# The head of a conditioned residual kernel in another order: sums over x ahead of the condition copies, x weight's sums early

## The chip, the cores and the metric

The kernel runs on one core of a Trainium2 chip. The metric is the device time of one execution in microseconds (us); before the change three runs gave 977.57, 976.78 and 973.87, median 976.78. A core has five engines that run their own instruction lists in order and wait for each other by semaphores: PE (TensorE, matrix products), DVE (VectorE), ACT (ScalarE), POOL (GpSimd) and SP (SyncE, which here only starts transfers). POOL starts the indexed transfers (gathers of rows and the scatter of the output), SP the others.

## The reference, cut to what matters

```python
h = _ln(x, pw_g[pathway_ids], pw_b[pathway_ids])
h = _ln(h, cp_g[compartment_ids], cp_b[compartment_ids])
t = _ln(x, tm_g[time_steps], tm_b[time_steps])
m = x + _mlp_ln(memory_state, ...)[:, None, :]
n = x + _mlp_ln(noise_state, ...)[:, None, :]
r = x + _mlp_ln(resource_state, ...)[:, None, :]
s = _ln(x, ms_g[scale_type], ms_b[scale_type])
w = jax.nn.softmax(aw)
cat = jnp.concatenate([w[0]*h, w[1]*t, w[2]*m, w[3]*n, w[4]*r, w[5]*s], axis=-1)
return x + _mlp_ln(cat, int_W1, int_b1, int_W2, int_b2, int_g, int_be)
```

x has 16 x 512 tokens of 512 values, all in float32. `_mlp_ln` is silu(s W1 + b1) W2 + b2 with a layer norm behind it; for m, n and r its input has one row for each of the 16 batches ("conditions").

## The kernel before

**What it makes of the reference.** The product with `int_W1` is split by the six blocks of `cat`. The x in m, n and r goes through one weight, wx_ = w2 W1[2] + w3 W1[3] + w4 W1[4]; t and s are the same normalized x with different row tables, so they go through one weight that depends on a token's group (time step and scale type: 15 groups). For that the kernel sorts all tokens by group, and takes them in 16 tiles of 512 tokens, each of four rows g of 128. What a token adds by its group and batch is a row of a small table, gathered and added. Rows of 128 tokens in which two groups meet are put right by "extra" tiles e0 and e1, whose products change those table rows.

**Stages.** First come loads, index arithmetic and a sort's loop of one-hot products (L815 to L819), up to about 33 us of the trace. Behind that loop everything is done in *pieces*, short closures with names, and three strings say in which order they are issued: `ORDER` for the head (conditions, tables, extra tiles, all of tile 0 and the most of tiles 1 and 2), `WINDOW` once for each tile, and `LAST`. The order in a string is the order of the instructions on every engine, since the schedule is by hand (`tc.manual_schedule()`, L501). `run` (L1212) takes the names one after the other:

```python
for name in names.split():
    ...
    if name not in done:
        done.add(name)
        piece(name)
```

A name is `kind.tile.index`; `e0` and `e1` stand for the extra tiles. The kinds that the text uses, with their lines and engines:

- `gx` (L200, POOL) gathers 128 rows of x into `xbs`; tile 0's four gathers come ahead of `ORDER` (L845). `gh` (L205, POOL) gathers a row of `pw` and one of `cp`.
- `xs` (L233, ACT) two passes over 128 rows of x for mean and variance, `xe` (L242, DVE), `xp` (L246, POOL) the power of -0.5 into `rsx`, `xm` (L254, DVE) `nmx`. `xn`, `nv` (L278, L272, ACT) the normalized x.
- `f1`, `fp`, `f2`, `fn`, `th` (L281 to L305) the second layer norm for h on DVE, POOL, DVE, ACT, and its transpose into `rH`; `tv`, `tx` the transposes into `rV`, `rX` (all DVE, L182). `sV.w.g`, `sH`, `sX`, `sZ`, `sE` (L187, SP): four transfers that spread row g of a transposed tile into `cV`, `cH`, `cX`, `cZ`, `cEe`. The transposed tile of e0 shares its room with `rX`.
- `xt`, `xv` (L951, L957): for tile 0, x is transposed on PE and copied by DVE.
- `sp` (L213, ACT) and `bd` (L222, DVE): the weight `vs` of row g, each four instructions; there are two such buffers.
- `lX`, `lV`, `lH` (L315, PE, products at L320): layer 1 of row g, one group of products for each block; `ga`, `ha`, `hs`, `tz` gather what is added, add, silu, transpose; `l2` (L336, PE) layer 2.
- `h2.s` (L964, PE) the second products of condition s, `he.s` (L969, ACT) their copies, `eh.s` (L978, PE) sums of quarters, `cv` (L1017, PE) the condition vectors `pv`; then `cs` (L1022, DVE), `cp` (L1029, POOL, `rsc`), `cn` (L1037, DVE), `ct` (L1040, PE), `ca` (L1045, DVE).
- `wk.s.c` (L947, DVE) adds block c of the x weight's part s into `wx_`. `lh` (L880, SP) loads `wh_`, `wh` (L995, ACT) scales it; `lw` (L1161, SP) loads `w2`; `lt` (L876, SP) three small tables.
- `tb`, `cm` (L1008, L1050, PE): products into `pb`, the table of additions; `cr` (L1057, ACT) copies it, `rp`, `rc`, `ro` pick and store its rows. `dp`, `dc`, `do` make the difference rows that `gr` gathers for the extra tiles; `mt`, `tr` (DVE) multiply and transpose them.
- `sz`, `scl` (L983, L1003): scales of the tiles on PE and ACT. `ax`, `ac`, `pwi`, `bx`, `by`, `kd`, `px`, `tk`: indices.
- `ex.k` (L1107, PE, `pe`) an extra product, `ea.k` (L1113, POOL, `adde`) the rows to be changed, `ee.k` (L1117, DVE) their sum, `eo.k` (L1120, SP) its storing. `xa` (L1070, DVE) and `ar` (L1128, DVE, 16 small instructions) make indices for `ea` and `ga`.

**What holds an instruction back.** Its operands, a free buffer (four PSUM slots for most of the head's small products, three for `pw` and for `cp`), and whatever stands ahead of it in its engine's list. A gather on POOL that waits for a buffer stops the powers behind it as well.

Of the kernel before, what the change touches and what calls it, by code (L numbers as in the profile page):

```python
# [17 lines left out]


ORDER = """  # L20
    sz scl bx lt ax wk.1.3 h2.1 ac sp.0.0 h2.2 lh he.2 cv h2.0 he.0 wk.1.1 pk se eh.2 eh.0 lw by pwi kd px dk he.1
    eh.1 wk.1.0 gh.0.2 xs.0.1 xs.0.0 dp wk.1.2 tk xt.0.2 xt.0.3 cg gh.0.0 gh.0.1 xs.0.3 xt.0.1 cs wk.2.2 xv.0.2
    xt.0.0 cp gx.e1.3 gx.e0.1 tt wk.2.0 cn xs.0.2 xv.0.3 xe.0 xv.0.1 dc wh gx.e1.2 xp.0 xv.0.0 ct xm.0 xn.0.2
    gx.e0.0 ca f1.0.2 nv.0.1 xn.0.1 wk.2.1 tb fp.0.2 cm do xn.0.0 wk.2.3 lX.0.1 gx.e0.2 f2.0.2 f1.0.0 fp.0.0 nv.0.2
    fn.0.2 xs.e0.1 xn.0.3 lo lX.0.3 tv.0.2 nv.0.0 nv.0.3 th.0.2 gh.0.3 lX.0.0 tv.0.1 cr rp.1 f2.0.0 fn.0.0 f1.0.1
    tv.0.0 tv.0.3 xs.e0.0 fp.0.1 f2.0.1 th.0.0 xs.e0.2 sp.0.1 gx.e0.3 xs.e0.3 gr.e0.2 sV.0.2 f1.0.3 gx.e1.0 fp.0.3
    lX.0.2 bd.0.1 f2.0.3 gx.e1.1 sV.0.1 fn.0.1 rp.0 xe.e0 th.0.1 fn.0.3 xp.e0 xs.e1.3 gr.e0.3 th.0.3 xs.e1.0 xm.e0
    nv.e0.3 sV.0.0 bd.0.0 gr.e0.0 sV.0.3 mt.e0.3 tr.e0.3 xa sH.0.1 nv.e0.2 mt.e0.2 rc.1 xs.e1.2 lV.0.1 xs.e1.1 xe.e1
    lV.0.0 tr.e0.2 gr.e0.1 gx.1.2 nv.e0.0 mt.e0.0 lH.0.1 nv.e0.1 rc.0 sp.0.3 sH.0.0 xp.e1 gr.e1.0 sH.0.3 xm.e1
# [22 lines left out]
    lV.c.1 sZ.p.3 q7.p.0.1 f1.c.2 f2.c.2 lX.c.3 xs.n.0 gx.n.2 f2.c.3 gx.n.3 fp.c.3 sp.c.2 fn.c.3 bd.c.2 fp.c.2  # L52
    fn.c.2 q7.p.0.2 sZ.p.2 po.o.2 sZ.p.1 sh.c.1 tx.n.1 ga.c.2 th.c.2 zs.p.4 xs.n.2 lV.c.2 xs.n.3 xe.n th.c.3 zs.p.5
    q7.p.1.5 sp.c.3 bd.c.3 tx.n.2 sH.c.1 q7.p.1.1 lV.c.3 lH.c.1 xp.n xm.n xn.n.0 nv.n.0 po.o.3 tx.n.0 kf.p.0 sp.n.0
    kf.p.2 zs.p.6 kf.p.3 zs.p.0 sH.c.0 zs.p.1 nv.n.3 ga.c.1 q7.p.1.7 sH.c.3 zs.p.7 sp.n.1 q7.p.1.3 sH.c.2 zs.p.2
    tx.n.3 nv.n.1 ga.c.0 q7.p.1.6 ku.p.1 tv.n.0 f1.n.0 ha.c.1 q7.p.0.5 sX.n.2 q7.p.1.2 q7.p.0.6 tv.n.3 sf.p.3 tv.n.1
    bd.n.0 zs.p.3 sf.p.2 gh.n.1 ga.c.3 sX.n.3 kf.p.1 fp.n.0 sf.p.0 q7.p.1.4 nv.n.2 xn.n.1 q7.p.0.7 sl.p.2 tv.n.2
    lH.c.0 sl.p.3 lq.p.2 sf.p.1 hs.c.1 ku.p.0 q7.p.0.4 gh.n.2 lq.p.3 f1.n.1 f2.n.0 sh.c.2 ha.c.0 q7.p.0.3 fn.n.0
    hs.c.0 sX.n.0 sX.n.1 sl.p.0 sh.c.0 sl.p.1 lq.p.0 sV.n.1 fp.n.1 th.n.0 f2.n.1 tz.c.0 lq.p.1 sh.c.3 lv.p lH.c.2
    ha.c.2 fn.n.1 lH.c.3 lp.p th.n.1 tz.c.1 lb.p.0 hs.c.2 sV.n.0 gh.n.3 sV.n.2 po.p.0 lb.p.2 lb.p.1 gx.m.0 gx.m.1  # L60
    po.p.1 sV.n.3
# [12 lines left out]
"""


# [1210 lines left out]
```

## Time and profile before

| what | before |
|---|---|
| runs | 973.87, 976.78, 977.57 us |
| span of the profiled execution | 973.856 us (the page shows no time beside the span) |
| granted TensorE clock, mean | 0.990 |
| PE busy | 946.2 us, 97% |
| DVE / POOL / ACT busy | 861.0 / 658.9 / 569.6 us |
| HBM read / written | 102.31 / 19.94 MB |

Times in the views are microseconds from the span's start. A row of the timeline reads: start, time, engine, line, operation, written tile <- read tiles, shapes, number of instructions, and in brackets the idle time of the engine just before and what ended it. Where several semaphores were waited for, the one that came last in the profile is named. A row of the windows reads: stretch, length, busy time and (instructions) of PE, PEld (weight loads), DVE, ACT, POOL, the granted clock as a share of full speed, the busy share of the DMA engines, GB/s. The chain of waits follows the work that ended last back in time; a row of it reads start, time, what.

### The profile page before, as it was taken

How to read it: one execution, taken by the hardware profiler on the slowest of the kernel's cores; microseconds unless marked ns; L12 is line 12 of the kernel's file. 1: busy time of each engine (PE TensorE's matmuls, PEld its weight loads, DVE VectorE, ACT ScalarE, POOL GpSimd, SP SyncE). 2: the span in 40 equal slices, each digit the busy share in tenths (PEclk: the TensorE clock that was granted, in tenths of full speed). 3: DMA queues.
4: the chain of work that ended last, by engine and by line, in shares of the span. 5: the costliest groups of instructions: out<-in, count | busy, mean ns of one | idle time of the engine just before them, and what ended most of it. 6: DMA issues, size and time to landing. Idle time of an engine off the chain costs nothing.

```text
span 973.9 us, 11591 instructions
## 1 busy us (share of the span) xinstructions
PE 946.2 (97%) x2901; PEld 497.9 (51%) x2901; DVE 861.0 (88%) x1412; ACT 569.6 (58%) x1190; POOL 658.9 (68%) x697
## 2 busy tenths in 40 slices
...
GB/s 278 207 255 218 283 244 244 135 223 206 203 203 180 196 173 193 195 202 197 207 200 188 196 173 193 205 197 184 205 204 208 202 180 179 199 194 166 148 85 97
DMA packets 91885, 190.95 MB, mean 196 GB/s; under 512 B 25364, under 2 KB 25364, under 8 KB 91820
## 3 DMA queue, kind: packets, MB, share of 16 engines
...
q14 instruction: 41, 0.34, 0.1%
...
HBM read 102.31 MB, written 19.94 MB: 126 GB/s over the span
## 4 chain that ended last, share of the span: by engine, by line
PE 79%; DVE 11%; DMA 4%; ACT 3%; SPq 2%; issue 2%; POOLq 0%; ACTq 0%; DVEq 0%
PE p L320 57%; PE p L339 4%; PE pq_1b L406 4%; DVE vs L226 4%; PE pq_0b L406 4%; PE pq_0a L406 3%; PE pq_1a L406 3%; SPq L192 2%; PE pe L1110 1%; DMA cX<-rX 1%; DVE yb L433 1%; DVE vs L724 1%; ACT junk L238 1%; DMA cZ<-rZ 1%; DMA cH<-rH 1%
## 5 line engine op out<-in xcount | busy, mean ns | idle before, releaser
L320 PE MATMUL p<-wh__83,cH 128*128 128x512 f32 x512 | 227.3, 592 | 1.0 <-DMA cH<-rH 1.0
L320 PE MATMUL p<-wx__82,cX 128*128 128x512 f32 x512 | 224.9, 592 | 0.0
L320 PE MATMUL p<-vs,cV 128*128 128x512 f32 x504 | 223.7, 592 | 0.8 <-DVE rH L184 0.8
L226 DVE SCALAR_TENSOR_TENSOR vs<-wt,sct,vs 128x512 f32<-128x512 f32 x252 | 214.5, 912 | 0.0
L220 ACT ACTIVATE vs<-ws,scs 128x512 f32<-128x512 f32 x252 | 161.3, 710 | 3.4 <-PE p L320 2.4
L320 PEld LDWEIGHTS p<-wx__82,cX 128*128 128x128 f32 x512 | 97.2, 190 | 117.3 <-issue 111.3
L320 PEld LDWEIGHTS p<-wh__83,cH 128*128 128x128 f32 x512 | 97.2, 190 | 112.7 <-issue 107.8
L320 PEld LDWEIGHTS p<-vs,cV 128*128 128x128 f32 x504 | 95.7, 190 | 110.5 <-issue 87.1
L497 POOL DMA_INDIRECT out<-yb,tok x64 | 71.0, 1110 | 59.9 <-DVE yb L462 20.7
L292 POOL TENSOR_TENSOR rsh<-veh,mhalf 128x1 f32<-128x1 f32 x64 | 51.0, 798 | 75.9 <-DVE veh L288 75.1
L471 ACT ACTIVATE junk<-yb 128x512 f32<-128x512 f32 x64 | 40.4, 631 | 96.9 <-DVE yb L435 78.4
L158 POOL DMA_INDIRECT cp<-cp_rows,i_cp x64 | 68.7, 1073 | 27.4 <-issue 18.0
L327 ACT ACTIVATE add<-add 128x512 f32<-128x512 f32 x64 | 39.8, 622 | 80.5 <-DVE add L324 80.4
L158 POOL DMA_INDIRECT xbs<-in_x,tok x64 | 66.9, 1046 | 24.5 <-issue 15.7
L158 POOL DMA_INDIRECT add<-rows,i_add x64 | 70.3, 1098 | 17.3 <-issue 10.8
L309 POOL TENSOR_TENSOR xbs<-xbs,rows 128x512 f32<-128x512 f32 x64 | 80.7, 1272 | 0.7
L158 POOL DMA_INDIRECT pw<-in_pw,i_pw x64 | 66.3, 1035 | 18.0 <-issue 11.0
L238 ACT ACTIVATE junk<-xbs 128x512 f32<-128x512 f32 x72 | 45.2, 628 | 56.4 <-DMA xbs<-in_x,tok 54.9
L296 ACT ACTIVATE pw<-pw,rsh 128x512 f32<-128x512 f32 x64 | 44.5, 715 | 55.1 <-POOL rsh L292 26.9
L260 ACT ACTIVATE xn<-xbs,nmx,rsx 128x512 f32<-128x512 f32 x64 | 50.2, 804 | 45.3 <-DVE nmx L256 44.8
L324 DVE TENSOR_TENSOR add<-p,add 128x512 f32<-128x512 f32 x64 | 43.7, 685 | 29.5 <-PE p L320 25.1
L260 ACT ACTIVATE xm<-xbs,nmx,rsx 128x512 f32<-128x512 f32 x64 | 51.9, 810 | 13.9 <-DVE rV L184 11.8
...
## 6 DMA issues: line engine op xcount, KB each, us to landing
cV<-rV SPq DMA_DIRECT2D x256, 64.0 KB
cH<-rH SPq DMA_DIRECT2D x256, 64.0 KB
cZ<-rZ SPq DMA_DIRECT2D x256, 64.0 KB
...
```

Source lines behind the costliest of these rows:

```text
L158: nc.gpsimd.indirect_dma_start(dst, None, table, bass.IndirectOffsetOnAxis(ap=idx, axis=0), **kw)
L220: nc.scalar.activation(v[:, c], ws[:, c], AF.Identity, scale=scs[:, c, g, w : w + 1])
L226: nc.vector.scalar_tensor_tensor(v[:, c], wt[:, c], sct[:, c, g, w : w + 1], v[:, c], ALU.mult, ALU.add)
L238: nc.scalar.activation(junk, x, AF.Identity, accum_out=sums[:, 0, j : j + 1])
L260: nc.scalar.activation(t, st["xb"][:, j, :], AF.Identity, bias=st["nm"][:, j : j + 1], scale=st["rs"][:, j : j + 1])
L292: nc.gpsimd.tensor_tensor(rs, st.pop(("ve", j)), mhalf[:, :1], ALU.pow)
L296: nc.scalar.mul(pw[:, :D], pw[:, :D], st.pop(("rs", j)))
L309: nc.gpsimd.tensor_add(st["xb"][:, j, :], st["xb"][:, j, :], rows[:, 2, :])
L320: nc.tensor.matmul(st["p1", g], st["c" + blk][:, g, c, :], m[:, c, :], start=(blk == "X" and c == 0), stop=(blk == "H" and c == NC - 1))
L324: nc.vector.tensor_add(st["add", g], st["p1", g], st["add", g])
L406: nc.tensor.matmul(home, st["zp", p][k][:, c], at_["half"][k][:, c], start=False, stop=(c == 1), skip_group_check=True)
L497: nc.gpsimd.indirect_dma_start(out_rows, bass.IndirectOffsetOnAxis(ap=tok[:, j, w : w + 1], axis=0), yb[:, j, :], None)
```

## The change

`ORDER` gets another order of the same 427 names: none is added or taken away. `WINDOW` and `LAST` hold the same names in the same order as before and are only broken into lines elsewhere, which moves the line numbers behind them by one. Both orders in full:

```diff
-    sz scl bx lt ax wk.1.3 h2.1 ac sp.0.0 h2.2 lh he.2 cv h2.0 he.0 wk.1.1 pk se eh.2 eh.0 lw by pwi kd px dk he.1
-    eh.1 wk.1.0 gh.0.2 xs.0.1 xs.0.0 dp wk.1.2 tk xt.0.2 xt.0.3 cg gh.0.0 gh.0.1 xs.0.3 xt.0.1 cs wk.2.2 xv.0.2
-    xt.0.0 cp gx.e1.3 gx.e0.1 tt wk.2.0 cn xs.0.2 xv.0.3 xe.0 xv.0.1 dc wh gx.e1.2 xp.0 xv.0.0 ct xm.0 xn.0.2
-    gx.e0.0 ca f1.0.2 nv.0.1 xn.0.1 wk.2.1 tb fp.0.2 cm do xn.0.0 wk.2.3 lX.0.1 gx.e0.2 f2.0.2 f1.0.0 fp.0.0 nv.0.2
-    fn.0.2 xs.e0.1 xn.0.3 lo lX.0.3 tv.0.2 nv.0.0 nv.0.3 th.0.2 gh.0.3 lX.0.0 tv.0.1 cr rp.1 f2.0.0 fn.0.0 f1.0.1
-    tv.0.0 tv.0.3 xs.e0.0 fp.0.1 f2.0.1 th.0.0 xs.e0.2 sp.0.1 gx.e0.3 xs.e0.3 gr.e0.2 sV.0.2 f1.0.3 gx.e1.0 fp.0.3
-    lX.0.2 bd.0.1 f2.0.3 gx.e1.1 sV.0.1 fn.0.1 rp.0 xe.e0 th.0.1 fn.0.3 xp.e0 xs.e1.3 gr.e0.3 th.0.3 xs.e1.0 xm.e0
-    nv.e0.3 sV.0.0 bd.0.0 gr.e0.0 sV.0.3 mt.e0.3 tr.e0.3 xa sH.0.1 nv.e0.2 mt.e0.2 rc.1 xs.e1.2 lV.0.1 xs.e1.1 xe.e1
-    lV.0.0 tr.e0.2 gr.e0.1 gx.1.2 nv.e0.0 mt.e0.0 lH.0.1 nv.e0.1 rc.0 sp.0.3 sH.0.0 xp.e1 gr.e1.0 sH.0.3 xm.e1
-    nv.e1.1 tr.e0.0 ro.1 gr.e1.1 nv.e1.0 gr.e1.2 sp.0.2 ro.0 mt.e0.1 xs.1.2 tr.e0.1 sE.e0.0 gx.1.3 lH.0.0 nv.e1.2
-    bd.0.3 lV.0.3 mt.e1.0 sE.e0.3 gx.1.0 tr.e1.0 gx.1.1 lH.0.3 ex.0 mt.e1.1 xs.1.3 xs.1.0 xs.1.1 sE.e0.2 gr.e1.3
-    tr.e1.1 ar bd.0.2 sE.e0.1 mt.e1.2 tr.e1.2 ea.0 lV.0.2 gh.1.3 nv.e1.3 wm gx.2.2 ee.0 gh.1.2 xe.1 xp.1 tx.1.0 xm.1
-    tx.1.1 mt.e1.3 tr.e1.3 sh.0.2 sH.0.2 tx.1.2 gh.1.0 nv.1.0 xn.1.3 gx.2.0 wl.4 eo.0 xn.1.2 xn.1.0 f1.1.3 tx.1.3
-    ea.1 sE.e1.0 nv.1.3 ex.3 ea.3 sE.e1.2 ex.1 fp.1.3 f2.1.3 wl.1 tv.1.0 sp.1.0 f1.1.0 f1.1.2 f2.1.2 nv.1.1 xs.2.0
-    gx.2.1 ex.2 fn.1.3 ea.2 sE.e1.1 fp.1.0 lH.0.2 sX.1.2 ex.6 ea.6 f2.1.0 th.1.3 ee.3 gh.1.1 sX.1.1 xn.1.1 wl.0
-    sp.1.1 tv.1.1 ee.2 ex.5 sh.1.1 sX.1.3 fp.1.2 ee.1 xs.2.2 nv.1.2 tv.1.2 sh.1.0 gx.2.3 ea.4 fn.1.2 eo.1 ee.6
-    xs.2.1 tv.1.3 eo.3 f1.1.1 bd.1.0 ea.5 ex.4 fn.1.0 fp.1.1 sh.0.0 lX.1.2 xs.2.3 lX.1.3 ee.4 eo.2 sX.1.0 sh.0.3
-    sV.1.3 lX.1.1 sh.0.1 ee.5 sh.1.3 lX.1.0 xe.2 th.1.0 th.1.2 eo.6 sV.1.0 eo.5 f2.1.1 tx.2.1 eo.4 bd.1.1 tx.2.2
-    wl.2 xp.2 fn.1.1 lV.1.0 tx.2.3 sp.1.2 sV.1.1 sV.1.2 th.1.1 lV.1.1 sH.1.1 tx.2.0 ga.0.0 xm.2 bd.1.2 lV.1.2 ga.0.2
-    sp.1.3 ha.0.2 hs.0.2 ga.0.3 ga.0.1 gh.2.0 ha.0.0 xn.2.0 gh.2.1 bd.1.3 hs.0.0 sH.1.3 xn.2.1 wl.3 ha.0.3 sH.1.0
-    lV.1.3 sX.2.0 tz.0.0 nv.2.3 sX.2.3 hs.0.3 ha.0.1 lH.1.3 hs.0.1 ga.1.1 sp.2.1 tz.0.3 tz.0.1 tz.0.2 sZ.0.1 nv.2.0
-    lH.1.0 gh.2.2 sp.2.0 f1.2.0 ga.1.0 lH.1.1 tv.2.0 f2.2.0 ga.1.2 f1.2.1 sZ.0.2 f2.2.1 wb nv.2.1 l2.0.1 fp.2.1
-    ga.1.3 sZ.0.3 bd.2.0 ha.1.0 nv.2.2 sZ.0.0 la.0.1 sH.1.2 fp.2.0 hs.1.0 tv.2.1 l2.0.3 tv.2.2 sX.2.1 l2.0.0 tz.1.0
-    ha.1.1 sX.2.2 fn.2.0 sh.1.2 la.0.0 l2.0.2 la.0.3 lq.0.0 th.2.0 tv.2.3 wq la.0.2 lq.0.1 lq.0.3 lq.0.2 lH.1.2
-    sV.2.1 lv.0 lp.0 fn.2.1 hs.1.1 sV.2.0 th.2.1 lb.0.0 ha.1.2 sV.2.3 hs.1.2 gh.2.3 po.0.0 tz.1.1 sV.2.2 lb.0.1
-    gx.3.0 lb.0.2 gx.3.1 po.0.1
+    xs.0.1 ax h2.2 h2.1 pk he.2 sz wk.1.2 wk.1.1 ac pwi xs.0.0 lw gh.0.0 wk.1.0 se wk.1.3 he.1 dk wk.2.2 gh.0.2 wk.2.3
+    eh.2 lt scl xt.0.2 bx wk.2.1 h2.0 xt.0.1 xv.0.2 tt wk.2.0 cv by gh.0.1 sp.0.0 he.0 eh.0 kd eh.1 dp xt.0.3 xv.0.1
+    xt.0.0 xs.0.3 px cs cp xs.0.2 xv.0.3 xe.0 cn tk xp.0 gx.e0.1 cg lh ct xm.0 xv.0.0 wh gx.e0.0 xn.0.0 tb xn.0.2 ca
+    nv.0.3 lo f1.0.0 sp.0.1 gx.e1.3 fp.0.0 gx.e0.2 f2.0.0 f1.0.2 fn.0.0 th.0.0 fp.0.2 f2.0.2 gh.0.3 xn.0.3 nv.0.1
+    xn.0.1 tv.0.3 dc nv.0.0 nv.0.2 tv.0.1 gx.e0.3 tv.0.0 xs.e0.1 xs.e0.0 cm do tv.0.2 lX.0.1 fn.0.2 cr lX.0.2 f1.0.1
+    lX.0.3 xs.e0.2 gx.e1.0 rp.0 fp.0.1 gx.e1.1 xs.e0.3 bd.0.1 rp.1 f1.0.3 xe.e0 gr.e0.1 lX.0.0 f2.0.3 gx.e1.2 sV.0.1
+    f2.0.1 xp.e0 th.0.2 rc.0 fp.0.3 xs.e1.3 xm.e0 sV.0.3 fn.0.1 fn.0.3 lV.0.1 nv.e0.1 gr.e0.2 th.0.1 nv.e0.2 sV.0.0
+    rc.1 th.0.3 xs.e1.0 gr.e0.3 bd.0.0 mt.e0.2 mt.e0.1 gx.1.1 xs.e1.2 tr.e0.1 gr.e0.0 nv.e0.3 ro.0 mt.e0.3 sH.0.0
+    nv.e0.0 xs.e1.1 gr.e1.1 ro.1 sp.0.3 tr.e0.3 xe.e1 tr.e0.2 mt.e0.0 lV.0.0 xp.e1 gx.1.0 xm.e1 gr.e1.0 lH.0.0 tr.e0.0
+    gr.e1.2 bd.0.3 nv.e1.0 sp.0.2 gx.1.2 nv.e1.2 sH.0.1 mt.e1.0 gx.1.3 nv.e1.1 xs.1.2 nv.e1.3 xs.1.3 gr.e1.3 sV.0.2
+    lH.0.1 mt.e1.2 tr.e1.2 xa ea.0 gh.1.0 mt.e1.3 lV.0.3 sE.e0.1 ex.1 xs.1.0 tr.e1.3 gh.1.3 mt.e1.1 sE.e0.0 tr.e1.0
+    ex.0 sH.0.3 sE.e0.3 lH.0.3 ee.0 xs.1.1 sE.e0.2 ar tr.e1.1 wm xe.1 xp.1 xm.1 eo.0 tx.1.0 sE.e1.2 tx.1.1 tx.1.3
+    xn.1.2 gx.2.0 xn.1.0 sE.e1.0 ea.2 ea.5 bd.0.2 sp.1.1 sE.e1.1 ex.2 wl.0 ea.3 sH.0.2 nv.1.0 ea.1 nv.1.1 gx.2.1
+    sh.0.2 bd.1.1 ee.2 tx.1.2 tv.1.0 nv.1.3 ee.1 tv.1.1 nv.1.2 wl.4 sX.1.2 gx.2.2 gh.1.2 ea.6 ex.3 lV.0.2 sX.1.0
+    sp.1.0 eo.2 ex.6 tv.1.3 f1.1.0 fp.1.0 ex.4 gx.2.3 tv.1.2 ex.5 xs.2.0 ee.3 f2.1.0 ea.4 bd.1.0 gh.1.1 f1.1.2 lH.0.2
+    lX.1.2 ee.5 xn.1.1 fn.1.0 xn.1.3 th.1.0 eo.1 sV.1.0 f1.1.3 sX.1.1 sh.1.0 fp.1.3 ee.4 ee.6 f2.1.2 sX.1.3 sh.1.2
+    eo.3 f2.1.3 xs.2.2 wl.2 fn.1.3 f1.1.1 tx.2.2 eo.5 lX.1.0 xs.2.1 f2.1.1 lV.1.0 sV.1.1 fp.1.2 eo.4 lX.1.1 fp.1.1
+    sp.1.2 fn.1.1 fn.1.2 eo.6 xs.2.3 ga.0.3 bd.1.2 th.1.1 ga.0.1 th.1.3 ga.0.2 sV.1.2 sV.1.3 xe.2 th.1.2 ga.0.0 xp.2
+    xm.2 xn.2.1 sH.1.0 ha.0.1 lV.1.1 lX.1.3 ha.0.3 hs.0.3 ha.0.2 ha.0.0 hs.0.1 tz.0.3 wl.1 sh.0.1 tz.0.1 sh.1.1 nv.2.2
+    gh.2.1 sH.1.1 hs.0.2 wb hs.0.0 ga.1.1 sh.0.3 tx.2.0 lV.1.2 tz.0.0 sp.1.3 xn.2.0 lH.1.0 tz.0.2 sH.1.2 wl.3 sZ.0.0
+    sp.2.0 tx.2.3 tv.2.2 nv.2.1 nv.2.0 lH.1.1 sZ.0.3 bd.1.3 gh.2.0 f1.2.1 tx.2.1 ha.1.1 lV.1.3 sh.0.0 tv.2.1 sZ.0.1
+    l2.0.3 ga.1.0 fp.2.1 l2.0.0 bd.2.0 gh.2.2 sH.1.3 nv.2.3 f2.2.1 l2.0.1 fn.2.1 f1.2.0 sX.2.0 ha.1.0 ga.1.3 fp.2.0
+    tv.2.0 sp.2.1 th.2.1 sZ.0.2 f2.2.0 la.0.3 la.0.1 l2.0.2 sh.1.3 sX.2.2 tv.2.3 la.0.2 sX.2.1 la.0.0 lq.0.0 lq.0.1
+    hs.1.1 lq.0.3 tz.1.1 lq.0.2 lH.1.2 sV.2.1 lH.1.3 fn.2.0 ga.1.2 lv.0 wq lp.0 th.2.0 ha.1.2 sV.2.3 sV.2.0 lb.0.1
+    gh.2.3 hs.1.0 tz.1.0 lb.0.2 lb.0.0 gx.3.1 hs.1.2 sV.2.2 po.0.0 sX.2.3 gx.3.0 po.0.1
```

By engine, with the places in the list (before, after):

- ACT: `xs.0.1` (30, 0) and `xs.0.0` (31, 11) ahead of the copies `he.2`, `he.1`, `he.0`; `xs.0.3`, `xs.0.2` behind them; `dc` (56, 85) behind the first norms.
- PE: `h2.2`, `h2.1` first, then `sz`, `eh.2`, the flip `xt.0.2`, `bx`, `h2.0`, `xt.0.1`, `cv`, `eh.0`, `eh.1`, `dp`, the other flips, `px`, `ct`, `tb`, `cm`. Behind them three groups `lX`, two `rp`, the fourth `lX`; then `lV.0.1`, `lV.0.0`, `lH.0.0`, `lH.0.1`, `lV.0.3`, `ex.1`, `ex.0`, `lH.0.3`, two more `ex`, `lV.0.2`, the three `ex` of e1, `lH.0.2`. The `l2.0` groups stand ahead of `lH.1.3` and `lH.1.2`.
- DVE: all eight `wk` ahead of `cs`; `tv.0` ahead of `f1.0.1`; `ee.0` ahead of `ar`, `tr.e1.1`, `tx.1` and `bd.0.2`; `xa` behind `bd.0.3`.
- POOL: `gh.0.0`, `gh.0.2`, `gh.0.1` in this order (2, 0, 1 before); `ea.0` behind the last `gr.e1`; `ea.2`, `ea.5`, `ea.3`, `ea.1` together.
- SP: `lw` ahead of `lt` and `lh`; `ro` between rows of `sV` and `sH`; for tile 0 `sZ.0.0`, `sZ.0.3`, `sZ.0.1` ahead of all `sX.2`, where two of `sX.2` stood ahead of `sZ`.

36 lines of the change are left out of this document (18 added, 18 removed).

## The prediction

> **What bounds the kernel now.** I read the page first, then busy time by windows, then PE's timeline for the waits in front of its matmuls.
>
> ```profile
> span 973.9 us, 11591 instructions
> 100.00:120.00 20.00, 19.33 (x46) 8.43 (x45) 13.76 (x35) 15.38 (x36) 12.72 (x13) 1.00 0.95 279
> 300.00:500.00 200.00, 199.31 (x570) 105.11 (x569) 188.04 (x293) 120.55 (x248) 145.23 (x144) 1.00 0.69 193
> ```
>
> Columns: stretch, its length, then busy PE, PEld, DVE, ACT, POOL, granted clock, DMA share, GB/s. From 300 to 500 us PE is busy 199.31 of 200: the windows are bound by PE, and the change does not touch them. It can act only on the head, and there only on two things: when the dense layer-1 products begin, and how long PE waits after that.
>
> ```profile
> 56.89 1.84 PE L1012 MATMUL pb<-wt,room 128*32 128x512 f32 x8 [0.19 <-ACT dr L942]
> 64.09 10.57 PE L320 MATMUL p<-wx__82,cX 128*128 128x512 f32 x24
> 80.58 7.11 PE L320 MATMUL p<-vs,cV 128*128 128x512 f32 x16 [0.78 <-DVE rH L184]
> 88.73 7.10 PE L320 MATMUL p<-wh__83,cH 128*128 128x512 f32 x16 [1.04 <-DMA cH<-rH]
> 103.38 3.67 PE L1110 MATMUL pe<-ws,cEe 128*128 128x512 f32 x8 [0.67 <-DMA cEe<-rEe]
> 125.59 10.54 PE L1110 MATMUL pe<-wt,cEe 128*128 128x512 f32 x24 [1.38 <-DVE sth L163]
> 175.20 13.97 PE L339 MATMUL p<-w,cZ 128*128 128x512 f32 x32 [1.31 <-DMA cZ<-rZ]
> 238.27 1.13 PE L406 MATMUL pq_0b<-w2t,cZ 128*128 128x256 f32 x4 [0.24 <-DVE yb L424]
> ```
>
> The dense work (lX) starts at S = 64.09. Behind it stand waits of 0.78 + 1.04 + 0.67 + 1.38 + 1.31 + 0.24 = 5.42 us, and otherwise matmuls end to end. So the gain is (64.09 - new S) + (5.42 - new waits). The second bracket can give at most 5.42, and no bound holds the losses.
>
> **The change part by part.** Nothing is computed more or less; every piece keeps its instructions. Durations therefore come straight from rows, and only starts move.
>
> *ACT before the dense work.* Four sums over x (xs) stood behind the condition copies (he), and `wh` and the first norm behind them.
>
> ```profile
> 36.20 1.88 POOL L158 DMA_INDIRECT xbs<-in_x,tok  x1 [5.53 <-DVE room L789]
> 38.38 0.95 POOL L158 DMA_INDIRECT xbs<-in_x,tok  x1 [0.30 <-issue]
> DMA to landing us min/median/max: 4.5/4.5/4.5
> 37.46 0.31 ACT L813 COPY g_at<-pgt 64x192 f32<-64x192 f32 x1 [0.64 <-PE pgt L804]
> 48.46 0.58 ACT L971 COPY ev<-po 128x512 f32<-128x512 f32 x1 [0.23 <-PE hs L981]
> 48.94 0.63 ACT L238 ACTIVATE junk<-xbs 128x512 f32<-128x512 f32 x1
> 56.74 1.99 ACT L996 ACTIVATE wh__83<-wh__83,wx 128x2048 f32<-128x2048 f32 x1
> ```
>
> ACT is free at 37.8 and now waits for x tile 1 ahead of everything. The first gather landed 4.5 after its issue, at 40.7, 2.6 behind the issue's end; the second ends its issue at 39.33, so 42.0 (42.9 if 4.5 is counted from its start; I take 42.0, as the first issue was long itself). One xs takes 1.84 (four of them and the 0.6 of `dr` fill 48.94 to 56.74). Queue: xs.0.1 to 43.8; he.2, ac 44.6; xs.0.0 46.4; he.1 47.0; scl 47.9; sp.0.0 50.4; he.0 51.0; two xs 54.7; wh 56.7. So `wh` is ready 2.0 earlier than 58.73, but the last he comes at 51.0 where it was 49.0. Behind that last he on PE stand cv, eh.0, eh.1 and with them cs, cn, ct, the whole condition chain.
>
> ```profile
> 52.05 0.95 POOL L158 DMA_INDIRECT cp<-cp_rows,i_cp  x1 [3.19 <-PE pdr L938]
> 53.02 0.73 POOL L1031 TENSOR_TENSOR rsc<-vec,mhalf 96x1 f32<-96x1 f32 x1
> 59.74 0.69 DVE L283 TENSOR_TENSOR pw<-xn,pw 128x512 f32<-128x512 f32 x1 [0.22 <-ACT xn L260]
> 50.05 0.17 DVE L925 CAST tok_x<-px 128x16 int32<-128x16 f32 x1 [3.27 <-PE px L832]
> 62.21 1.41 DVE L949 SCALAR_TENSOR_TENSOR wx__82<-w1x,wx,wx__82 128x512 f32<-128x512 f32 x2
> ```
>
> On POOL the second cp gather waits for cv (`pv`), then a pw and a cp follow at 1.25 each: 51.3 to 55.0, so rsc's power ends at 55.75, cn at 56.3, ct at 57.0, tb begins at 57.1 (56.89 before). The products tb and cm took 56.89 to 64.09. New S = 64.3 at the same clock.
>
> ```profile
> 36.00:38.00 2.00, 2.00 (x14) 1.86 (x14) 1.41 (x4) 0.76 (x5) 1.80 (x1) 0.64 0.03 8
> 44.00:46.00 2.00, 2.00 (x12) 0.34 (x4) 1.84 (x10) 1.22 (x3) 1.28 (x2) 0.50 0.81 272
> 46.00:48.00 2.00, 2.00 (x14) 0.66 (x13) 0.79 (x2) 0.79 (x2) 1.09 (x2) 0.80 0.79 201
> 56.00:58.00 2.00, 1.66 (x12) 0.74 (x16) 1.45 (x4) 2.00 (x4) 1.67 (x3) 0.76 1.08 394
> 58.00:60.00 2.00, 2.00 (x12) 0.44 (x8) 1.05 (x4) 1.84 (x3) 1.68 (x2) 0.50 0.89 215
> ```
>
> The granted clock was one half from about 36.6 to 46.8 and again from 57.0 to about 60.5. At full clock in the second stretch tb would be 3.4/2 = 1.7 shorter: S = 62.6. The other bound is the second half-clock stretch running on from 46.8: I put S = 66.5 there (64.3; 1.2 more for some 1.2 of products on the path between 51 and 57 that would take twice as long; 1.0 for one more stretch of 3.4, partly used). The value taken is 64.1, no gain, since the pieces just ahead of tb are as thin as before.
> [...]
>
> ```profile
> 71.57 1.29 DVE L184 STREAM_TRANSPOSE rV<-xm 128x512 f32<-128x512 f32 x2
> 79.88 1.56 DVE L184 STREAM_TRANSPOSE rH<-pw 128x512 f32<-128x512 f32 x2
> 83.13 6.87 SPq L192 DMA_DIRECT2D cH<-rH  x11
> 97.57 5.67 DMA cEe<-rEe
> 107.51 0.69 DVE L1118 TENSOR_TENSOR adde<-pe,adde 128x512 f32<-128x512 f32 x1 [0.55 <-DMA adde<-rows,i_addx]
> 100.34 0.94 POOL L158 DMA_INDIRECT adde<-rows,i_addx  x1 [0.30 <-DMA pre<-diff_rows,tok_x]
> 99.33 0.15 DVE L852 CAST sib<-at_n 128x64 int32<-128x64 f32 x1
> 102.89 2.73 DVE L226 SCALAR_TENSOR_TENSOR vs<-wt,sct,vs 128x512 f32<-128x512 f32 x4
> 116.19 7.52 SPq L192 DMA_DIRECT2D cEe<-rEe  x12
> ```
>
> *x weight's sums (wk) and DVE.* The last two blocks of wx_ (row 62.21, 1.41) went ahead of cs, into DVE's gap of 3.27 before tok_x in 47 to 50; the w2 load likewise went ahead of lt and lh on SP, under a DMA share that is 0.03 at 36 to 38. Both cost nothing there; without that gap the blocks would delay cs by up to 1.4. Since rsx's power now stands behind rsc's, nmx comes at 57.0, ca ends at 58.5, and f1 begins there and not at 59.74. DVE then is 1.24 + 1.41 = 2.65 ahead until about 77, where it loses 1.6 to fn.0.1, late on ACT behind four xs of the extra tiles. Transposes to rV come before f1.0.1 now: rV is whole at about 68 (72.9 before), rH at 80.3 (81.4).
>
> *The waits behind S.*
> 0.78 (lV): rV and build 1 are whole by 73: gone. 1.04 (lH): SP is free when rH is whole and sends one row of cH from 80.4, where it began at 83.13: gone.
>
> 0.67 (first extra product): rEe is whole some 4.5 earlier, its first row lands at 98.7, but the product moved up by one group of eight matmuls (3.43; four of them are the 13.97 at 175.20) and PE is 1.8 ahead (the two waits that went): wanted at 97.5, wait 1.2. 1.38 (second extra tile): ee.0 now stands on DVE ahead of ar (3.6, rows 99.33 to 102.89), tr.e1.1, tx.1 and bd.0.2, a new wait with all these queued behind it. ee.0 needs ex.0 (PE, about 104.5) and its gather's landing (7.2 from 100.34 to 107.51 before). At 104.7 the rows of cEe are in time; at 107 they come 1.7 late; I take 0.8.
> 1.31 (layer 2): l2 moved ahead of lH.1.3 and is wanted 3.43 + 2.5 earlier; on SP the eight sends of cX went behind cZ.
>
> ```profile
> 160.34 6.68 SPq L192 DMA_DIRECT2D cX<-rX  x8
> 167.12 12.04 SPq L192 DMA_DIRECT2D cZ<-rZ  x16
> 168.98 6.08 DMA cZ<-rZ
> ```
>
> That is 6.68 earlier by the queue and some 2 by rH; less 2.5, since the row wanted first is now sent second: 6 against 5.9 needed, wait about 1.0 (bounds 0 and 4). With 0.24 left, the waits sum to 1.2 + 0.8 + 1.0 + 0.2 = 3.2.
>
> Sum: (64.09 - 64.1) + (5.42 - 3.2) = 2.2 us off the profiled span of 973.9: 971.7. The median of the runs shown, 976.78, lies 2.9 above that span (the lowest, 973.87, on it), so the median to expect is 974.6.
>
> **The rivals.**
> *All waits go.* For it: the order moves the late senders forward (cZ ahead of cX on SP, eo.0 ahead of the second extra tile). Against it: landings of 5.7 to 6.1 where DMA is 0.95 busy. With S = 62.6 to 64.1 and waits of 0.2 the gain is 5.2 to 6.7: 970.8.
> *The clock stays low.* S = 66.5, other waits as above or smaller, because PE then comes later to each: gain about -0.2 to 0.5: 977.
> *Slower: DVE stuck at ee.0.* Place: DVE's queue in 100 to 120. From ee.0's start to the first chunk of bd.0.2 lie 0.65 + 3.6 + 0.65 + 1.3 (vea, power, nmx) + 1.9 + 0.7 = 8.8. If ee.0 starts at 107.5 as before, lV.0.2 can start at 116.3; by then PE has done 15.7 for lX and the two pr and ten groups, 50 in all; before, it had as much behind it at 64.09 + 50 + 2.5 of waits = 116.6. So 107.8 is the point: each us later is a us lost. Its index piece xa moved behind bd.0.3 and two extra tiles on DVE, and the gather stands behind eleven POOL items that wait for buffers. Issued at 105 with 7.2 to land it costs 4.5 and moves the second extra tile too, about 1: 982. Against it: xa by my queue is done at 96.
> *It does nothing* (every us returned at l2, where cZ waits for its own chain): 976.8.
>
> **How the numbers follow.** Forecast (gain 0.5 to 4.9) 0.42; all waits go 0.23; clock stays low 0.10; nothing 0.07; DVE stuck 0.18. A measurement here tells about 0.5%, 4.9 us, from none; so faster 0.23, same 0.59, slower 0.18. The forecast's own range is 972 to 977. For 8 in 10 I reach to 969.5 (6.7 gained, and 0.6 for the scatter of the median) and up to 982 (the DVE rival).
>
> **What would show it.** Right: the first xs on ACT at 42, the last he at 51, lX at 63 to 65, no wait before lV and lH, short waits at the first pe, the second extra tile and l2 summing to 2 to 4. Wrong: lX after 66 or before 62; ee.0 on DVE after 108 with a wait for adde; a wait over 4 at l2; or any wait in front of a layer-1 group of tile 1, where I counted none.

## The result, and the profile after

The first set of runs gave 980.75 us for the changed kernel (14 runs, 977.51 to 985.15) and 976.56 us for the kernel before (14 runs), a ratio of 1.0041, 95% interval [1.0026, 1.0056]. Two more sets gave 1.0005 [0.9991, 1.0019] and 1.0040 [1.0023, 1.0058]. Over all three sets the medians are 979.54 (38 runs) and 976.77 us (69 runs). So the change makes the kernel about 0.3% slower; I had forecast 0.2% faster. Some 0.3 us of the difference lies outside the traces: in each of the 38 runs the time is 2.1 to 2.2 us above that run's span, with the kernel before 1.7 to 1.9; no view shows what it is. Medians of one kernel differ between sets (the kernel before: 975.5 to 977.9), so kernels of different sets are compared by their ratios to it.

In the changed kernel's profile all lines behind `ORDER` have numbers lower by one; in the experiments they are those of before. First PE's timeline of the changed kernel, the same columns as before:

```profile
span 980.9 us, 11595 instructions
45.44 1.88 PE L980 MATMUL hs<-ev,sel 128*32 128x512 f32 x2 [2.95 <-DVE sel L975]
67.69 10.57 PE L319 MATMUL p<-wx__82,cX 128*128 128x512 f32 x24
102.00 3.70 PE L1109 MATMUL pe<-wt,cEe 128*128 128x512 f32 x8 [0.67 <-DMA cEe<-rEe]
136.73 7.03 PE L319 MATMUL p<-wx__82,cX 128*128 128x512 f32 x16
176.01 7.99 PE L338 MATMUL p<-w,cZ 128*128 128x512 f32 x18 [0.80 <-ACT w L1158]
184.48 3.67 PE L338 MATMUL p<-w,cZ 128*128 128x512 f32 x8 [0.47 <-DMA cZ<-rZ]
194.86 10.46 PE L319 MATMUL p<-wx__82,cX 128*128 128x512 f32 x24
222.61 1.13 PE L405 MATMUL pq_1b<-w,cZ 128*128 128x256 f32 x4 [1.61 <-POOL cZ L384]
232.94 1.13 PE L405 MATMUL pq_1b<-w2t,zs 128*128 128x256 f32 x4 [0.90 <-ACT yb L416]
237.06 1.13 PE L405 MATMUL pq_1a<-w,cZ 128*128 128x256 f32 x4 [0.29 <-ACT yb L427]
245.28 1.13 PE L405 MATMUL pq_0b<-w2t,cZ 128*128 128x256 f32 x4 [1.06 <-DVE yb L423]
253.98 6.60 PE L319 MATMUL p<-wx__82,cX 128*128 128x512 f32 x15
```

And four rows of the same view of the kernel before, the first layer-1 products of tile 1 and of tile 2, the fourth group of tile 2, and the first products of tile 3:

```profile
135.96 13.90 PE L320 MATMUL p<-wx__82,cX 128*128 128x512 f32 x32
192.44 10.46 PE L320 MATMUL p<-wx__82,cX 128*128 128x512 f32 x24
210.86 3.60 PE L320 MATMUL p<-wx__82,cX 128*128 128x512 f32 x8
246.96 10.46 PE L320 MATMUL p<-wx__82,cX 128*128 128x512 f32 x24
```

The row at 246.96 is tile 3's: the 24 products from 192.44 and the 8 from 210.86 are all 32 of tile 2's `lX`. Some expectations below call it "the fourth" of tile 2; their numbers are those from tile 2's first lX to tile 3's. Four stretches can be cut with these rows. The changed kernel begins lX 3.60 late (67.69 against 64.09); it needs 2.83 less to tile 1 (69.04 against 71.87), since the waits before lV, lH and the second extra tile are gone; 1.65 more to tile 2 (58.13 against 56.48); and 4.60 more to tile 3 (59.12 against 54.52), where waits stand that I had counted as none (1.61, 0.90, 0.29, 1.06, and 0.19 of a smaller one). From there to the end both take 726.9. So the whole difference, 7.0 us in these two profiles, is made by 254 us.

The late lX has a first sign in the idle 2.95 before `hs`. DVE's and ACT's timelines name it:

```profile
43.86 0.23 DVE L1000 CAST i_cp<-pa 128x64 int32<-128x64 f32 x1 [4.90 <-ACT at_n L886]
41.44 0.63 ACT L237 ACTIVATE junk<-xbs 128x512 f32<-128x512 f32 x1 [4.07 <-DMA xbs<-in_x,tok]
```

The first sum over x waits 4.07 for its rows on ACT; `ac` (at_n) stands behind it, `pwi` on DVE waits for `ac`, and behind `pwi` stand an x weight block and `sel` (44.00 to 45.29), without which no `hs` can start.

### The profile page after: what moved, and what is told of

Its sections match the earlier page's. It is cut to its first block, busy times and chain, and to the rows that moved or that the text cites. A ratio compares the mean times of both kernels' runs of the same rounds, so it can differ in the third digit from the quotient of the medians.

```text
span 980.9 us, 11595 instructions
## 1 busy us (share of the span) xinstructions
PE 949.9 (97%) x2901; PEld 497.5 (51%) x2901; DVE 859.8 (88%) x1412; ACT 568.4 (58%) x1190; POOL 659.9 (67%) x697
## 4 chain that ended last, share of the span: by engine, by line
PE 74%; DVE 9%; DMA 6%; POOL 5%; issue 3%; ACT 3%; SPq 0%; POOLq 0%; DVEq 0%; ACTq 0%
PE p L319 54%; PE pq_0b L405 4%; PE pq_1b L405 4%; PE pq_1a L405 3%; PE pq_0a L405 3%; PE p L338 3%; DVE vs L225 2%; DMA rows<-adde 2%; DMA xbs<-in_x,tok 1%; DVE yb L432 1%; POOL add L157 1%; PE pe L1109 1%; DVE vs L723 1%; ACT junk L237 1%; POOL xbs L308 1%
## 5 line engine op out<-in xcount | busy, mean ns | idle before, releaser
L225 DVE SCALAR_TENSOR_TENSOR vs<-wt,sct,vs 128x512 f32<-128x512 f32 x252 | 209.4, 891 | 0.0
L496 POOL DMA_INDIRECT out<-yb,tok x64 | 71.0, 1110 | 66.5 <-DMA out<-yb,tok 21.1
L291 POOL TENSOR_TENSOR rsh<-veh,mhalf 128x1 f32<-128x1 f32 x64 | 50.2, 785 | 68.5 <-DVE veh L287 67.9
L157 POOL DMA_INDIRECT xbs<-in_x,tok x64 | 65.9, 1030 | 24.2 <-issue 16.9
L157 POOL DMA_INDIRECT add<-rows,i_add x64 | 70.5, 1102 | 14.8 <-issue 10.4
L295 ACT ACTIVATE pw<-pw,rsh 128x512 f32<-128x512 f32 x64 | 44.3, 715 | 56.3 <-POOL rsh L291 28.0
```

Source lines behind the costliest of these rows:

```text
L157: nc.gpsimd.indirect_dma_start(dst, None, table, bass.IndirectOffsetOnAxis(ap=idx, axis=0), **kw)
L225: nc.vector.scalar_tensor_tensor(v[:, c], wt[:, c], sct[:, c, g, w : w + 1], v[:, c], ALU.mult, ALU.add)
L291: nc.gpsimd.tensor_tensor(rs, st.pop(("ve", j)), mhalf[:, :1], ALU.pow)
L295: nc.scalar.mul(pw[:, :D], pw[:, :D], st.pop(("rs", j)))
L496: nc.gpsimd.indirect_dma_start(out_rows, bass.IndirectOffsetOnAxis(ap=tok[:, j, w : w + 1], axis=0), yb[:, j, :], None)
```

## The experiments

Below, lX without a tile is the first layer-1 group of tile 0 that runs. The table has the cut for the profiles that the text compares most; each entry is the difference of two starts as in the rows above, "to the end" the span less the start of tile 3.

| profile | lX | to tile 1 | to tile 2 | to tile 3 | to the end | lX to the end |
|---|---|---|---|---|---|---|
| before | 64.09 | 71.87 | 56.48 | 54.52 | 726.9 | 909.8 |
| new start, old rest (e7, e18) | 62.88, 64.42 | 71.45, 72.30 | 57.82, 57.77 | 54.95, 55.10 | 726.2, 725.9 | 910.4, 911.1 |
| changed (first, e13, e17) | 67.69, 63.92, 64.85 | 69.04, 69.40, 69.05 | 58.13, 59.41, 59.60 | 59.12, 58.00, 58.26 | 726.9, 726.7, 727.0 | 913.2, 913.5, 914.0 |
| la and scatter early (e5) | 67.47 | 69.24 | 58.97 | 56.82 | 727.8 | 912.8 |
| la early (e14) | 62.51 | 69.52 | 59.56 | 59.16 | 726.4 | 914.6 |
| scatter early (e15) | 62.84 | 69.61 | 60.18 | 56.15 | 726.4 | 912.4 |
| mended start, old rest (e8, e16) | 63.40, 65.90 | 70.62, 69.53 | 58.40, 56.63 | 54.89, 55.25 | 725.4, 728.2 | 909.3, 909.6 |

### Is it the start?

Two local repairs of the changed kernel:

```diff
-    xs.0.1 ax h2.2 h2.1 pk he.2 sz wk.1.2 wk.1.1 ac pwi xs.0.0
+    ax ac xs.0.1 h2.2 h2.1 pk he.2 sz wk.1.2 wk.1.1 pwi xs.0.0
```

> The changed kernel, with ax and ac alone moved ahead of xs.0.1, so that on DVE i_cp (and the two wx_ blocks and sel behind it) no longer waits until 43.86 for a copy that stands behind the first sum over x. Theory A (the stop on DVE costs PE's start): i_cp before 41.5, sel whole before 43.2, the first hs product at 43.8 (then it waits for he.2 on ACT) where it is at 45.44, PE idle there 1.3 where it is 2.95, dense layer 1 (lX) at 66 if the half-clock stretch keeps its 10.2 us, at 64 if it becomes shorter, where it is 67.69; the time 1.6 to 3.6 below that of the changed kernel (980.75), so 977 to 979. Theory B (the granted clock alone makes lX late, whatever hs waits for): hs at 43.8, but lX still at 67 to 68 and 980 to 981.

```diff
-    xs.0.1 ax h2.2 h2.1 pk he.2 sz wk.1.2 wk.1.1 ac pwi xs.0.0
+    ax h2.2 ac he.2 xs.0.1 h2.1 pk sz wk.1.2 wk.1.1 pwi xs.0.0
```

> The changed kernel, with ac and the copy he.2 moved ahead of xs.0.1 (into the 4.07 us in which ACT waits for the first rows of x): the first hs product waits for nothing. Theory A: he.2 on ACT at 39.7, hs right behind psc at 42.5 without idle time, lX at 63.5 to 65, the time 2.7 to 4.2 below the changed kernel, 976.5 to 978. Theory B: hs at 42.5, PE still at half clock for 10 us of what follows, lX at 66 to 68 and 979 to 981. A third theory, that an earlier lX is lost again at layer 2 of tile 1 (222 to 246): lX at 64, but waits of 6 to 7 us in 212 to 250 in place of 4.05, and 980 to 981.

e1 did to `hs` what was expected (43.79, with 1.43 of idle), and lX began at 64.34; but the ratio to the kernel before stayed 1.0042 [1.0018, 1.0066]. e2: lX at 60.48, ratio 1.0025 [1.0001, 1.0050]; waits of 1.57 (for cH, tile 1) and 1.92 (for cZ, layer 2) came behind it. A start 7.2 earlier in the profile was worth 3.9 of span. The start alone, behind it the old order:

```diff
     xt.0.0 xs.0.3 px cs cp xs.0.2 xv.0.3 xe.0 cn tk xp.0 gx.e0.1 cg lh ct xm.0 xv.0.0 wh gx.e0.0 xn.0.0 tb xn.0.2
-    ca nv.0.3 lo f1.0.0 sp.0.1 gx.e1.3 fp.0.0
+    gx.e1.3 dc gx.e1.2 ca f1.0.2 nv.0.1 xn.0.1 fp.0.2
...
```

> The first 66 names of the new order (to the first ca), then the remaining names as in the kernel before: the new start alone. Theory A (the start costs 3.6 at lX, and the 5.4 of waits behind it in the old order take a part back): lX at 67 to 68.5, waits behind it 2 to 3.5 where they are 5.42, waits in 212 to 250 at most 0.5, the span 975.5 to 977.5, the median 977 to 978.5. If all the lateness is carried to the end: 979. If the waits take all of it back: 975 to 976.

```profile
62.88 10.57 PE L320 MATMUL p<-wx__82,cX 128*128 128x512 f32 x24
134.33 13.90 PE L320 MATMUL p<-wx__82,cX 128*128 128x512 f32 x32
192.15 10.46 PE L320 MATMUL p<-wx__82,cX 128*128 128x512 f32 x24
247.10 10.46 PE L320 MATMUL p<-wx__82,cX 128*128 128x512 f32 x24
```

That is PE's timeline of e7: the same instructions up to `tb` as in the changed kernel, and lX at 62.88, not at 67 to 68.5. The ratio was 0.9984 [0.9966, 1.0001]. So the same kernel, and then this one, went again:

> The changed kernel once more, for a second profile of it and as a measure beside the three others on one chip. Theory C (where lX begins is set by where the half-clock stretches fall, and that differs between executions): S is near 63 if the clock first drops at about 35.5, and near 67.5 if it drops at 37 to 37.6, as the five executions of this start so far; the waits in 212 to 250 are 3 to 4.5 either way. Theory A (the new order itself makes lX 3.6 late): S 67 to 68 whatever the clock's times.

> The changed kernel a third time. The first set of runs put it 0.41% above the kernel before, the second (e13) 0.05%. If the true difference is near 0.25%, between 0.1 and 0.4% above; lX between 62.5 and 67.7, by where the clock drops (67 to 67.7 only if its first drop lies at 37 to 37.7); waits in 212 to 250 of 2.5 to 4.5.

> The new start with the old rest, as e7. If the new start itself costs nothing and all of the loss stands behind it: level with the kernel before or up to 0.2% below, and 0.2 to 0.5% below the changed kernel of e17. If the start costs: above the kernel before by 0.1 to 0.3%, level with e17.

The changed kernel began lX at 63.92 in e13 and 64.85 in e17, and e18 gave 0.9994 [0.9979, 1.0009] beside 1.0040 for e17 on the same chip. So beside the old start the first 66 names of the new order cost nothing that the runs show, and the loss comes with what stands behind them. What differs between the executions is the granted clock. Busy times by windows, of the first profile of the changed kernel, of e13 and of e7, one fence each (columns as in the prediction):

```profile
44.00:48.00 4.00, 2.56 (x6) 0.89 (x6) 3.86 (x13) 3.90 (x10) 2.16 (x2) 0.55 1.04 393
60.00:64.00 4.00, 4.00 (x24) 0.98 (x20) 3.83 (x9) 4.00 (x7) 2.99 (x4) 0.50 0.54 146
```
```profile
44.00:48.00 4.00, 3.01 (x10) 1.05 (x10) 3.86 (x12) 3.91 (x9) 2.06 (x2) 0.50 1.01 398
60.00:64.00 4.00, 4.00 (x45) 1.21 (x37) 3.83 (x8) 3.92 (x8) 3.12 (x4) 1.00 0.69 181
```
```profile
44.00:48.00 4.00, 3.27 (x30) 2.13 (x30) 3.86 (x13) 3.97 (x9) 1.79 (x2) 0.73 1.01 341
60.00:64.00 4.00, 4.00 (x39) 1.49 (x32) 3.83 (x8) 2.93 (x6) 3.41 (x4) 1.00 0.86 292
```

In the first profile the table products ran at half clock from 60 to 64 (0.50), in the other two at full clock (1.00). In the first profile's record of the granted clock the changes lie at 37.61, 41.02, 44.44, 54.68, 58.09 and 64.92, in that of the kernel before at 36.57, 46.81, 57.05 and 60.46: the steps are 3.41 us or 2 or 3 times that. For the ten profiles that have this start (e10, e4, e7, e13, e18, e5, the first one, e17, e14, e15):

| first drop to half clock | 35.39 | 35.44 | 35.57 | 36.03 | 37.06 | 37.27 | 37.61 | 37.90 | 38.00 | 38.39 |
|---|---|---|---|---|---|---|---|---|---|---|
| lX | 62.87 | 62.86 | 62.88 | 63.92 | 64.42 | 67.47 | 67.69 | 64.85 | 62.51 | 62.84 |
| us at half clock before lX | 13.65 | 13.65 | 13.65 | 17.07 | 13.65 | 20.48 | 20.48 | 17.07 | 6.83 | 6.83 |

The times at half clock are 2, 4, 5 and 6 times 3.41, and the first drop lies between 35.39 and 38.39; what sets its place was not tested. One start, 5.2 us of spread, a mean of 64.2; the latest two are those with the most time at half clock. The first profile was the worst. Theory A fell: the stop on DVE is real, but it does not make the kernel slower by what the first profile showed.

### Is it the end of the order?

The table says that the stretch from tile 2's first lX to tile 3's takes 54.5 to 55.3 with the old rest and 58.0 to 59.1 in the changed kernel, wherever lX begins. The chain of waits of the changed kernel, first profile, shows through what (rows between these are left out):

```profile
202.57 1.01 POOL out L496
203.89 4.44 DMA xbs<-in_x,tok
212.31 6.31 DMA xbs<-in_x,tok
228.85 0.80 ACT xm L259
232.36 0.25 ACT yb L414
236.76 0.26 ACT yb L427
237.06 1.13 PE pq_1a L405 x4
```

POOL's timeline of the changed kernel and then of the kernel before, the scatters of tile 0 (`out`) and the third gather of tile 3 (`xbs`):

```profile
202.57 1.01 POOL L496 DMA_INDIRECT out<-yb,tok  x1 [1.56 <-DVE yb L492]
207.50 1.48 POOL L496 DMA_INDIRECT out<-yb,tok  x1 [2.43 <-DMA out<-yb,tok]
212.31 0.95 POOL L157 DMA_INDIRECT xbs<-in_x,tok  x1 [0.30 <-issue]
```
```profile
195.96 1.01 POOL L497 DMA_INDIRECT out<-yb,tok  x1 [0.30 <-issue]
201.02 1.29 POOL L497 DMA_INDIRECT out<-yb,tok  x1 [1.45 <-DMA out<-yb,tok]
205.20 1.02 POOL L158 DMA_INDIRECT xbs<-in_x,tok  x1 [0.30 <-issue]
```

In the new order the scatters wait 1.56 (for the last of three `lb` on DVE) and 2.43 (for the first scatter) with gathers behind them, before 0 and 1.45. Tile 3's third gather goes 7.1 later, 4.7 of it beyond the 2.4 by which PE is late there; in e13, where PE is 0.3 late at tile 2, it goes 4.5 later (209.70). Its rows feed the sums on ACT; the copies `yb` of tile 1's layer 2 stand behind them in ACT's list, and PE waits for these copies. Two repairs, together and singly:

```diff
-    l2.0.0 bd.2.0 gh.2.2 sH.1.3 nv.2.3 f2.2.1 l2.0.1 fn.2.1
+    l2.0.0 la.0.3 lq.0.3 bd.2.0 gh.2.2 sH.1.3 nv.2.3 f2.2.1 l2.0.1 la.0.0 lq.0.0 fn.2.1
...
-    f2.2.0 la.0.3 la.0.1 l2.0.2 sh.1.3 sX.2.2 tv.2.3 la.0.2 sX.2.1 la.0.0 lq.0.0 lq.0.1 hs.1.1 lq.0.3 tz.1.1 lq.0.2 lH.1.2
+    f2.2.0 la.0.1 lq.0.1 l2.0.2 sh.1.3 sX.2.2 tv.2.3 la.0.2 lq.0.2 lv.0 sX.2.1 hs.1.1 tz.1.1 lH.1.2
...
-    ga.1.2 lv.0 wq lp.0
+    ga.1.2 lp.0 wq
...
-    lb.0.1 gh.2.3 hs.1.0 tz.1.0 lb.0.2 lb.0.0 gx.3.1 hs.1.2 sV.2.2 po.0.0
+    lb.0.0 po.0.0 lb.0.1 gh.2.3 hs.1.0 tz.1.0 lb.0.2 gx.3.1 hs.1.2 sV.2.2
```

> The changed kernel, with the last steps of tile 0 (la, lq, lv, lp, and the scatter po.0.0 with its lb.0.0) moved ahead of tile 2's pieces at the end of the order; the start as changed. Theory E (the waits in 212 to 250 come from tile 0's la standing on DVE behind bd.2.0 and tile 2's second norm, which makes rsy, the scatters and tile 3's gathers on POOL some 4 us later than before): rsy at 191.5 to 193 where it is 195.89, the first zs on POOL at 217 to 218.5 where it is 221.03, waits in 212 to 250 of 0.5 to 2 where they are 4.05, the time 2 to 3.5 below the changed kernel: 977.3 to 978.8. Theory S (these waits are what a late start leaves over, and not this order): lX still at 67 to 68, waits of 3.5 to 4.5, 980 to 981.

e14 has the first three pieces of this edit, e15 the last:

> The changed kernel with only la, lq, lv and lp of tile 0 moved forward, as in e5; lb.0.0 and po.0.0 stay. If tile 0's sums on DVE are what costs at the end: 0.2 to 0.3% below the changed kernel (e13). If the scatter's wait on POOL is: less than 0.1% below.

> The changed kernel with only lb.0.0 and po.0.0 moved ahead of lb.0.1. If the scatter's place on POOL (ahead of both gathers of tile 3, waiting for the last lb) is what costs: 0.2 to 0.3% below the changed kernel (e13). If tile 0's sums on DVE are: less than 0.1% below.

POOL's timeline of e15 and, behind it, PE's; then PE's of e13, which ran in the same set and had tile 2's first lX at 192.73 where e15 had it at 192.63:

```profile
195.69 1.29 POOL L497 DMA_INDIRECT out<-yb,tok  x1 [2.28 <-DVE yb L493]
206.32 0.95 POOL L158 DMA_INDIRECT xbs<-in_x,tok  x1 [0.30 <-issue]
182.26 3.67 PE L339 MATMUL p<-w,cZ 128*128 128x512 f32 x8 [2.16 <-DMA cZ<-rZ]
240.08 1.13 PE L406 MATMUL pq_0b<-w2t,cZ 128*128 128x256 f32 x4 [1.18 <-DVE yb L424]
```
```profile
182.35 3.67 PE L339 MATMUL p<-w,cZ 128*128 128x512 f32 x8 [1.12 <-DMA cZ<-rZ]
219.26 1.13 PE L406 MATMUL pq_1b<-w,cZ 128*128 128x256 f32 x4 [0.38 <-POOL cZ L385]
229.69 1.13 PE L406 MATMUL pq_1b<-w2t,zs 128*128 128x256 f32 x4 [0.91 <-ACT yb L417]
242.04 1.13 PE L406 MATMUL pq_0b<-w2t,cZ 128*128 128x256 f32 x4 [1.07 <-DVE yb L424]
```

With the scatter early, the third gather goes at 206.32 and not 209.70, the waits for POOL's cZ and for ACT's yb are gone, and the stretch takes 56.15 and not 58.00. With only `la` early it takes 59.16: nothing gained. So by one profile of each the place of the scatter (with its `lb`) is a part of the loss, about 1.9 us, and tile 0's sums on DVE are not, against what I expected of e5. The runs cannot weigh it: e5 1.0011 [0.9994, 1.0029], e15 1.0013 [0.9994, 1.0031], e14 1.0038 [1.0024, 1.0053], beside e13 with 1.0005 in the set of e14 and e15. A part of the gain of e15 was lost again ahead of it, at layer 2 of tile 0 (2.16 for cZ, where e13 waits 1.12).

Both repairs together, start (as e2) and end (as e5):

> Both repairs: ac and he.2 ahead of xs.0.1 (as in e2_ac_he2_first) and tile 0's last steps early (as in e5_sums_out_early). If the two causes add: lX at 60 to 64, waits in 212 to 250 of 0.5 to 1.5 where e2 had 2.54, the median 1 to 2 below e2's 978.35: 976.3 to 977.3, level with the kernel before (975.5). If PE behind 64 only waits for other engines, whose work this does not make earlier: waits grow elsewhere (lH and layer 2 of tile 1, 150 to 182, by as much), 978 to 979.

0.9987 [0.9968, 1.0007], from 1.0025 for e2: no longer slower than the kernel before, though the two ran in different sets. Its profile is not what I expected: lX at 67.07 and not 60 to 64 (23.9 us at half clock before it), 57.34 from tile 2 to tile 3, with 2.55 of waits there. Then whole parts of the order were exchanged. The new end alone, behind the old order:

```diff
     nv.2.1 sZ.0.3 nv.2.2 sZ.0.0 sH.1.2 tv.2.1 tv.2.2 ha.1.1 sh.1.2
+    l2.0.3 ga.1.0 fp.2.1 l2.0.0 bd.2.0 gh.2.2 sH.1.3 nv.2.3 f2.2.1 l2.0.1
...
```

> The kernel before, with its last part (the 61 names that in the new order run from l2.0.3 to the end) in the new order; start and middle as before. Theory E (the order of the end costs by itself): from the first lX of tile 2 to the fourth 56.5 to 59 us where the kernel before takes 54.5, waits of 1.5 to 4 in 212 to 250 where it has 0.24, and the time 0.15 to 0.4% above the kernel before. Theory S (the waits there only follow from a late start, or from the new middle): 54.5 to 55, and no difference.

1.0058 [1.0041, 1.0075], but not where I expected it: the stretch of tile 2 took 53.74, and 62.96 the one ahead of it. PE's timeline and the windows of e9:

```profile
185.53 5.37 PE L339 MATMUL p<-w,cZ 128*128 128x512 f32 x8 [4.57 <-DMA cZ<-rZ]
```
```profile
184.00:188.00 4.00, 2.47 (x3) 1.05 (x4) 2.56 (x4) 0.00 (x0) 2.73 (x3) 0.71 0.98 270
```

The last row of cZ goes late, PE waits 4.57, and the clock falls to one half at its end. This wait is at least in part made by the seam, where the two orders meet: SP sends `sZ.0.2` behind eight sends of cH (5.02 us), where the changed kernel has four (2.49) there and PE waits 0.47 to 1.12. So e9 does not say what the new end costs by itself. The old end behind the new middle, cut at two places (e4, e10):

```diff
     sh.0.0 sh.1.3
+    lV.1.2 ga.0.2 sp.1.3 ha.0.2 hs.0.2 ga.0.3 ga.0.1
...
```

```diff
     sh.1.3 lH.1.3 sX.2.3
+    ga.1.1 sp.2.1 tz.0.3 tz.0.1 tz.0.2 sZ.0.1
...
```

> The names of the new order without the last 102 names of the old one, and these behind them as in the old order: the new start and middle with the old end. Theory A: lX at 67 to 68 as in the changed kernel; waits in 212 to 250 at most 0.6 where they were 4.05; the start of the fourth group of layer 1 of tile 2 about 2.4 behind the kernel before (246.96) and not 7.0; span about 976.5, median 978 (2.4 less than 980.75 to 3.5 less). If the waits in 212 to 250 follow from the late start and not from the order of the end: they stay at 3 to 4.5 and the median at 980 to 981.

> The new start and middle, with the last 75 names of the old order (ga.1.1 to the end) behind them in the old order. Theory E: 54.5 to 55.5 us from the first lX of tile 2 to the fourth (59.1 in the changed kernel), and the time 0.3 to 0.5% below the changed kernel, so between 0.1% below and 0.1% above the kernel before. If the loss sits in the middle: 0.2% or more above the kernel before.

e12 is e10 with the mended start of e2:

> The mended start (ac and he.2 ahead of xs.0.1), the new middle, the old end (as in e10). If middle and mended start add: 0.7 to 0.9% below the kernel before. If the middle gives nothing beside e8_mended_start_old_rest: 0.5 to 0.7% below. If it costs: less than 0.4% below.

The old start ahead of the new middle and end (e3), and with the old end of e10 too (e11):

```diff
     tb fp.0.2 cm do xn.0.0 wk.2.3
+    nv.0.3 lo f1.0.0 sp.0.1 fp.0.0 gx.e0.2 f2.0.0 fn.0.0 th.0.0
...
```

> The first 76 names of the old order (up to the last table product and the first lX), then the remaining names in the new order: the old start with the new middle and end. Theory A: lX at 63.5 to 65; no wait before lV and lH, as in the changed kernel; at the first pq_0a about 1.2 ahead of the kernel before (209.6), so 208.4; the waits in 212 to 250 stay at about 4, since they come from the end of the order; the span 976 to 977.5, the median 977 to 978. If the waits in 212 to 250 were a consequence of the late start: below 1.5 us there, span 972 to 973, median 974 to 975.5.

> The first 76 and the last 75 names in the old order, all between them in the new one. If the middle brings what I forecast for it (no waits at lV, lH and the second extra tile) and keeps it: 70 us from lX to tile 1's first lX where the kernel before takes 71.9, and 0.15 to 0.3% below it. If it is given back in layer 1 and layer 2 of tile 1 (136 to 192): 58 to 60 us there where the kernel before takes 56.5, and no difference, up to 0.2% above.

All of these were slower, e3, e4 and e11 by more than any case that I had written down: e4 1.0072 [1.0047, 1.0096], e10 1.0087 [1.0064, 1.0110], e12 1.0068 [1.0039, 1.0096], e11 1.0091 [1.0070, 1.0113], e3 1.0045 [1.0025, 1.0065]. With the old end the stretch of tile 2 was 53.7 to 55.1 in e4, e10, e11 and e12, as the theory of the end has it (e9, with the new end behind a long wait, had 53.7 too), but at the seam tile 1's last weight came late on DVE: waits of 8.08 (e4), 5.83 (e10), 4.52 (e11) and 5.04 us (e12) before an lV of tile 1. In e3 the seam is at the start, and 1.57 are lost there before an `rp`. So they do not say what the middle is worth by itself; that stays open.

One measure orders all twenty profiles, e9 too: how long behind tile 2's first lX the third gather of tile 3 is issued (205.20 - 192.44 in the kernel before).

| third gather behind tile 2's first lX | from tile 2 to tile 3 | profiles |
|---|---|---|
| 12.3 to 13.3 | 53.7 to 55.3 | before, e4, e7 to e12, e16, e18 |
| 13.7 | 56.15 | e15 |
| 14.8 to 15.3 | 56.3 to 57.6 | e2, e3, e5, e6 |
| 15.8 | 57.9 | e1 |
| 16.9 to 17.9 | 58.0 to 59.2 | changed (first, e13, e17), e14 |

Together with the chain above and e15 this says what lengthens the stretch behind tile 2 in the traces: the late gather. What the 1.7 to 3.1 us between tile 1 and tile 2 come from was not tested.

### A kernel that beats both

The mended start of e2 (its first 66 names) and the old rest, as in e7:

> The mended start of e2_ac_he2_first (66 names; ac and he.2 ahead of xs.0.1), then the remaining names as in the kernel before. If PE is the bound behind lX: lX at 60.5 to 64, 0 to 3.5 earlier than the kernel before, and so much off the time: 972 to 975.5. If behind lX other engines set the pace: the waits behind lX grow from 5.42 to 7 to 9, and the median is 975 to 976.5, as before.

> The kernel of e8_mended_start_old_rest again, since seven runs carried its verdict. If it is the better kernel: 0.4 to 0.8% below the kernel before. If e8 was a lucky set of clocks: 0 to 0.3% below.

0.9933 [0.9908, 0.9958] and 0.9972 [0.9957, 0.9987]: faster than the kernel before in both sets, 972.58 and 975.31 us. The second, 0.28%, lies in the 0 to 0.3% that I had given to a lucky first set, so the size of the gain is not settled. Their two profiles (972.7 and 975.5) have lX at 63.40 and 65.90 and 909.3 and 909.6 behind it, as before. So the gain, seen only in the medians, is not located by a profile. It goes with the mended start: in the set of e5 to e8, e8 with it has 972.58 and e7 without it 977.11, and e6 with it 977.03 and e5 without it 980.10.

## Why the prediction was wrong

**The begin of lX** was put at 64.1, between 62.6 and 66.5. Over ten profiles it was 62.5 to 67.7, mean 64.2: the bounds were a little narrow, and that the value is met is luck. The first product of `tb` began at 57.0 to 59.5 for my 57.1, and from there to lX it took 5.5 at full clock and up to 8.2 at half clock, for my 7.2. The choice of 64.1 was my estimate, from pieces ahead of `tb` that are as thin as before; no run shows that their thinness sets the clock. In the runs one order of these pieces had 6.8 to 20.5 us at half clock before lX, so neither the 64.1 nor the 66.5 of the clock rival is a value of the order. The old start's four profiles, of before, e3, e9 and e11, have 58.7 to 64.8, mean 62.7; at the same 13.65 us at half clock it has 64.09, 64.79 and 63.24, the new start 62.86 to 64.42. ACT's queue was read rightly up to the first xs (41.44 for 42.0). The last `he` came at 51.70 for 51.0, but not through that queue:

```profile
51.70 0.58 ACT L970 COPY ev<-po 128x512 f32<-128x512 f32 x1 [2.38 <-PE po L966]
```

ACT was free at 49.3 and waited 2.38 for the products `h2.0`, which PE ran late; the stop on DVE behind `ac`, 4.90, was overlooked.

**lV, lH and the extra tiles.** In the first profile and in e17 the two waits are gone (e13 has 0.97 before an lH), the second extra tile waited for nothing in the first profile, and the stretch to tile 1 was 2.5 to 2.8 shorter, for which I had 1.9 (0.78 + 1.04 + 1.38 + 0.67 less 1.2 and 0.8). Right.

**Layer 2 of tile 0** was to wait 1.0 in place of 1.31. In the three profiles of the changed kernel it waits 1.27, 1.12 and 1.79 (cZ, and in two of them 0.80 for the last of four passes of ACT over w2, L1159, which I had not counted). Ahead of it stand waits of 0.72, 1.98 and 1.16 before lV and lH of tile 1, where I had counted none and had named any as a sign of being wrong. The stretch took 1.7 to 3.1 more than in the kernel before.

**The failed step** is "With 0.24 left, the waits sum to 1.2 + 0.8 + 1.0 + 0.2 = 3.2": I followed each queue to `l2` and no further, and carried the 0.24 over. Behind tile 2's first lX came 4.05, 2.93 and 3.18 us of waits, and 3.5 to 4.6 more time. In the traces this goes with tile 3's third gather, issued 16.9 to 17.5 behind that lX and not 12.8; a scatter that waits ahead of it on POOL is a part of the delay (e15: 13.7, and 1.9 us less), and the rest of the delay was not singled out. With the waits before lV and lH of tile 1, the changed kernel takes 3.4 to 4.2 more behind lX than the kernel before, where I had 2.2 less.

**The rivals.** DVE at ee.0 did not decide: it ran at 109.18 with nothing to wait for, in a profile where lX was 3.6 late, and at 106.09 and 106.55 in e13 and e17. That all waits go, or that nothing happens, did not come. An lX as late as the clock rival had it, past 66.5, was in the first profile and in e5, and in none of the other eight with this start: an event of an execution. The forecast's own range, 972 to 977, did not hold the 980.75; the wider one, to 982, did, but its upper end was there for the stop at ee.0, which did not come: luck. The sign was wrong.
